# An LSTM kernel on one Trainium2 core: U sums on VectorE, bias differences in result buffers, streamed products from step 6, step 7's plain products ahead of step 0

## Chip, core and metric

The kernel runs on one core of one Trainium2 chip. The metric is the device time of one execution in microseconds (us), less is better. The kernel before takes 3121.33 us (median of three runs, 3120.87 to 3123.91).

In the profile PE is TensorE's matmul stream, PEld its weight loads, DVE is VectorE, ACT is ScalarE, POOL is GpSimd, and SPq is the queue of the Sync engine, from which every DMA of this kernel is issued. L245 is line 245 of the kernel before.

## What is computed

An LSTM over 512 steps, batch 32, input width and hidden width 512, all float32, with the input added to the output:

```python
def step(carry, xw_t):
    prev_h, prev_c = carry
    a = xw_t + prev_h @ Wh
    i = sigmoid(a[:, :Hd]); f = sigmoid(a[:, Hd:2*Hd])
    o = sigmoid(a[:, 2*Hd:3*Hd]); g = tanh(a[:, 3*Hd:])
    next_c = f * prev_c + i * g
    next_h = o * tanh(next_c)
    return (next_h, next_c), next_h

xW = einsum('ntd,dg->ntg', x, Wx) + b          # all steps: [32, 512, 2048]
hs = scan(step, (h0, 0), xW over the steps)
out = x + hs
```

So there are two products: the recurrent one, `prev_h @ Wh`, which must be made step by step, and the input product `x @ Wx`, which can be made at any time before its step.

## The kernel before, in words

**Layout.** A step's gates are a tile of 128 partitions (4 blocks of hidden units x 32 batch rows) by 512 columns, one PSUM bank. Eight banks are used: `xbank_0` to `xbank_4`, `bbank`, and `gbank_0`, `gbank_1`. From step 9 on a step's gates lie in `gbank[t % 2]`; the first nine steps have banks of a list (`bank_of`), step 7 has `xbank_3` and step 8 has `xbank_4`.

**A step.** `h_part(t)` (L245) adds the recurrent product to the step's bank. `cell(t)` reads the bank with ScalarE (L260 to L262), makes the new state on VectorE (L264 to L271, with a tanh of ScalarE, L267, between), transposes h for the next recurrent part (`ht`), and adds x for the output on GpSimd (L279). TensorE fills the time of the cell with input products.

**Input products, in two ways.** Steps 0 to 19 (the head, `HEAD = 20`) and the last 12 get *plain* products: x of one step against Wx as it is (`plain_block`, L178, 64 matmul rows for a step). Steps 20 to 499 are taken in 20 groups (`NG`) of 24 steps (`GS`), each with a fast bilinear scheme of 20 slots (`R`): each slot is a sum of x blocks (U) times a sum of weight blocks (V), seven 128x256 products a slot, and the results are added together to the outputs (W sums). These are the *streamed* products (`emit_matmuls`, L523). Their order is a list, `items`: row n of it has product 1 and 5 of slot n, 6 and 3 of slot n-1, 7 and 2 of slot n-2, and 4 of slot n-3. A position in the stream counts quarters of products, so 12 is three products; group 0 has 560.

- The U sums are made by `u_op` (L425) into six buffers `ubuf`, `u_ahead` deciding how far ahead. The sums of pairs of x blocks that they start from are made by `pair_sum` (L484 to L490) after `load_group` has brought a group's x into `xs0` or into `xs1`, which is the place of the weights Wx, free once the last plain product of the head is done.
- The V sums are made on VectorE in steps 0 to 4 (`v_slot`, L673), stored to DRAM (`v_store`, L685), and read back row by row into a ring of three (`load_v`, L602), two rows ahead of the stream. The buffers in which they are made are the ring itself and `ubuf`.
- Slot s uses bank `xbank[s % 5]` and half of `bbank`. Results are copied out by `evacuate` (ScalarE L569, L578, L585; VectorE L575, L579, L582) into eleven buffers `cbuf`, handed out from the list `free_c`. A product whose bank part has not been copied out yet has to wait (`needs`).
- The W sums (`w_op`, L389) are 1024 columns wide, in place in the `cbuf` buffers. A finished output block is stored to DRAM (L405) and read back into `xw` three steps before its step (`load_xw`, L614 and L620); `seed_step` (L631) copies it to the step's bank.
- Six slots (1, 3, 8, 11, 13, 17) start from a combination of biases: `seed_banks` (L553) copies it from a seed tile to the slot's bank. Two of the six combinations lie in `seeds_own`, the four others (`seeds[0]` to `seeds[3]`) in `r1[:, 6:8]`, the place of weights that plain products read.

**Where head plain products go.** Steps 0 to 4 are made before step 0 (`KEPT = 5`). The other 15 are made during steps 0 to 7 by the list `HEAD_PLAINS`, each ahead of its time. `keep(p)` adds the bias: in the bank itself, or into `xw[p % 3]`, or, from step 14 on, into one of six halves of `cbuf[8]` to `cbuf[10]` (`parks`), from which it is stored to DRAM (`kept_stores`, L784). The products of a step that has no bank of its own yet go to one of three banks in turn: `xbank_1`, `xbank_2`, `bbank` (`park_bank`).

**What sets the order.** The order on each engine is the order of the program text; nothing is reordered. In steps 0 to 15 (`HEAD_STEPS`) a step's work is a list of chunks, plain steps and pieces of the stream, and the cell is emitted after the first chunk. Jobs for VectorE (`jobs`) are spread over the plain chunks of their step. `room["dve"]` is a budget of VectorE time: TensorE's work adds to it, each operation takes its cost from it, and a W sum is emitted only while over 800 is left. SP issues its DMAs in program order too, and waits there for whatever the next one needs.

**The head before.** The stream begins in step 7, after the last plain step. U sums of the head and the pair sums of group 1 run on GpSimd. Raw biases are loaded in step 5 to three halves of `parks` (`load_raw_seeds`, L748); GpSimd takes their differences (L752) and, one step after the last plain product, makes three of the four late seeds in `r1[:, 6:8]` (L756 to L758), ScalarE copies the fourth (L759).

Of the kernel before, what the change touches and what calls it, by code (L numbers as in the profile page):

```python
# [28 lines left out]
TAU = (1, 0, 2)  # L29
NS = NG * R  # L30
KEPT = 5
STRAIGHT = 11
PARKED = 14
AHEAD = 28
STREAM0 = HEAD + GS - AHEAD
END = HEAD + GS * NG - AHEAD
SPLIT = END + 2
LATE = (454, 456, 458, 460, 462, 470, 471)

HEAD_PLAINS = ((14, 15), (6, 16), (5, 17), (7, 18), (8, 19), (11, 12), (9, 13), (10,))  # L40
V_DIRECT = (0, 2, 6, 9, 18, 19)
V_FIRST = (1,)
V_STEPS = ((3, 4, 5), (7, 8, 10), (11, 12, 13), (14, 15), (16, 17))
# [54 lines left out]
def kernel(  # L98
# [193 lines left out]

    free_c = [*range(8), 10, 8, 9]
    last_x = []
    free_u = list(range(6))
    room = {"dve": 0.0}
# [5 lines left out]
    def flat(a):  # L304
        return a.rearrange("p a b -> p (a b)")
# [110 lines left out]
    def u_block(gr, i):  # L416
        if i < 6:
            return flat(xs[gr.g % 2][:, i, 1:8])
        return flat(ubuf[:, gr.u[i]])

    def u_op(gr, terms):
        (a, sa), (b, sb) = sorted(terms.items(), key=lambda v: -v[1])
        dst = take(free_u)
        eng = nc.gpsimd if in_head[0] else nc.vector
        (eng.tensor_add if sb > 0 else eng.tensor_sub)(flat(ubuf[:, dst]), u_block(gr, a), u_block(gr, b))  # L425
        if not in_head[0]:
            room["dve"] -= cost_dve(896)
        for i in (a, b):
            if i > 5:
                gr.u_uses[i] -= 1  # L430
                if gr.u_uses[i] == 0:
                    free_u.append(gr.u[i])
        return dst

    u_made = [0]
    in_head = [True]

    def make_sum(gr, i):
        if i > 5 and i not in gr.u:
# [36 lines left out]
            in_=xg[g].rearrange("p (k s m) -> p k s m", k=6, s=4),  # L476
        )

    def pair_sum(g, i, eng=nc.vector):
        z = xs[g % 2]  # L480
        add, sub = eng.tensor_add, eng.tensor_sub
        a21, a11, a12, a22, s1, s2, s3, s4 = (z[:, :, n] for n in range(8))
        if i == 0:
            add(s1, a21, a22)  # L484
# [257 lines left out]
    def early_seeds():  # L742
        split_seeds((4, 5))
        sub(seeds[5], seeds[5], seeds[4])

    def load_raw_seeds():
        for i in range(3):
            nc.sync.dma_start(out=parks[i], in_=bias[i : i + 1].to_broadcast([P, W]))  # L748

    def split_raw_seeds():  # L750
        for q in parks[0:3]:
            nc.gpsimd.tensor_sub(q[:, HW:W], q[:, HW:W], q[:, 0:HW])  # L752

    def late_seeds():
        q = parks
        nc.gpsimd.tensor_add(seeds[3], q[2], seeds[4])  # L756
        nc.gpsimd.tensor_sub(seeds[2], q[2], q[0])
        nc.gpsimd.tensor_sub(seeds[1], q[1], q[0])  # L758
        nc.scalar.copy(seeds[0], q[0])  # L759

    parks = [cbuf[:, 8 + i // 2, i % 2 * 2 : i % 2 * 2 + 2].rearrange("p s c -> p (s c)") for i in range(6)]
    park_banks = [xbank[1], xbank[2], bbank]
# [7 lines left out]
        return park_banks[parked.index(p) % 3]  # L772

    def keep(p):
        if p < STRAIGHT:
            add(bank_of(p), bank_of(p), bias_full)
            return
        if p < PARKED:
            add(xw[:, p % 3], park_bank(p), bias_full)
            return  # L780
        n = p - PARKED
        dst = parks[n % 6]
        add(dst, park_bank(p), bias_full)
        kept_stores.append(lambda: nc.sync.dma_start(out=kept[n], in_=dst))  # L784

    with tc.manual_schedule():
# [4 lines left out]
        for c in range(4):  # L791
            ko, ki = divmod(c, 2)
            nc.sync.dma_start(
                out=r1[:, 4 * ko : 4 * ko + 4, 2 * ki : 2 * ki + 2].rearrange("p j s c -> p j (s c)"),
                in_=wx[c].rearrange("p (j c) -> p j c", j=NJ),
            )
        for j in range(NJ):
            nc.sync.dma_start(
                out=bias_full[j * B : (j + 1) * B], in_=bias[j : j + 1].to_broadcast([B, W])
            )  # L800
# [36 lines left out]
        HEAD_STEPS = STREAM0  # L837
        head_work = (HEAD - KEPT) * PLAIN + (R * 7) * PROD
        done_work = 0.0
        n_plain = 0  # L840
        group_loaded = 1
        plains_done = T
        s_done = {0: 4}
        v_ready = False
        plain_tail = []
# [4 lines left out]

        for t in range(T):
            h_part(t)
            for f in stores + kept_stores:
                f()
            stores.clear()
            kept_stores.clear()
            store_blocks()
            c, rest = divmod(t + 6, TC)
            if rest == 0 and 3 <= c < NCHUNK - 1:
# [9 lines left out]
            if t == 3:  # L869
                load_x(2, 4, 8)  # L870
                load_seeds(((4, 3), (5, 1)), nc.sync)
                load_group(0)
            if t == 5:
                load_raw_seeds()
            if PARKED <= t + 3 < HEAD + NG * GS:
                load_xw(t + 3)

            if t < HEAD_STEPS:
                target = head_work * (t + 1) / HEAD_STEPS
                chunks = []  # L880
                for p in HEAD_PLAINS[t] if t < len(HEAD_PLAINS) else ():
                    chunks.append(("plain", p))
                    n_plain += 1
                    done_work += PLAIN
                n = 4 * int((target - done_work) / PROD + 0.5) if n_plain == HEAD - KEPT else 0
                if t == HEAD_STEPS - 1 and n:
                    n = R * 7 * 4 - pos[0]
                left = n
                while left > 0:
                    m = min(left, 12 if chunks else 24)  # L890
                    chunks.append(("stream", m))
                    left -= m
                done_work += n * PROD / 4
                todo = jobs.pop(t, [])
                plains = sum(k == "plain" for k, _ in chunks)
                for i, (kind, m) in enumerate(chunks):
                    if kind == "plain":
                        bank = bank_of(m) if m < STRAIGHT else park_bank(m)
                        room["dve"] = 3000.0
                        for cc in range(4):  # L900
                            plain_block(m, cc, bank)
                        if i == 0:
                            cell(t)
                            if t + 1 >= STRAIGHT:
                                seed_step(t + 1)
                        keep(m)
                        if n_plain == HEAD - KEPT:
                            plains_done = t
                        last = i == plains - 1
                        for _ in range(len(todo) if last else -(-len(todo) // (plains - i))):  # L910
                            todo.pop(0)()
                            flush_v()
                    else:
                        load_v_ahead()
                        u_ahead(m)
                        if i == 0:
                            room["dve"] = min(room["dve"], 1000.0) + PLAIN
                        evacuate()
                        if t >= HEAD_STEPS - 3 and dve_jobs:
                            dve_jobs.pop(0)()  # L920
                        u_ahead(m + 24)
                        while wqueue and room["dve"] > 800:
                            w_op()
                        seed_banks(m)
                        emit_matmuls(m)
                        room["dve"] += m * PROD / 4
                        if i == 0:
                            cell(t)
                            room["dve"] -= 2500.0
                            if t + 1 >= STRAIGHT:  # L930
# [12 lines left out]

# [5 lines left out]
            in_head[0] = False  # L949
# [95 lines left out]
```

## Time and profile before

| | |
|---|---|
| three runs, median | 3121.33 us (3120.87 to 3123.91) |
| profiled execution | 3121.53 us, span 3119.80 us, mean granted TensorE clock 0.999 |
| PE busy over the span | 3094.5 us, 99% |
| DVE / ACT / POOL busy | 2226.7 (71%) / 1452.0 (47%) / 282.0 (9%) us |
| DMA | 760.39 MB, mean 244 GB/s |

How to read the profile's rows. A line of the page's busy time by stretches gives the stretch, its length, and for each engine the busy time with the number of instructions, then the granted clock of TensorE as a share of full speed, the busy share of the 16 DMA engines, and GB/s. A line of the waits gives who waited for whom: us in total, times, the longest. A line of the timeline gives the start, the busy time, the engine, the line and operation, what is written and read, and how many instructions are merged in it; brackets hold the idle time before it and what ended it. The end of a matmul row is modelled, so distances are better taken from start to start. A line of the groups gives busy time and mean duration in ns, then the idle time before. A float32 matmul is two rows in the trace.

### The profile page before, as it was taken

Reading aid. Unit: us, or ns where it says so; the run is one execution under the profiler, and the core shown is the slowest. Engines: PE = TensorE matmul, PEld = TensorE weight load, DVE = VectorE, ACT = ScalarE, POOL = GpSimd, SP = SyncE. Lnnn points to the kernel's source line nnn. Section 1 sums busy time; section 2 is a strip of 40 time slices with the busy share of each in tenths; the row PEclk is TensorE's granted clock in tenths of the full one; section 3 lists DMA queues with packets and bytes.
Section 4 is the critical chain, followed back from the end, with each engine's and each line's share of the span. In section 5 each row is a group of like instructions: output and inputs, shape, how many; then the busy total and the mean of one; then the engine's idle time right before and its main releaser. Section 6 shows DMA issues by size and latency. Waiting matters only on the chain.

```text
span 3119.8 us, 109182 instructions
## 1 busy us (share of the span) xinstructions
PE 3094.5 (99%) x44064; PEld 1660.0 (53%) x44064; DVE 2226.7 (71%) x6192; ACT 1452.0 (47%) x5484; POOL 282.0 (9%) x533
## 2 busy tenths in 40 slices
PE   9989999999999999999999999999999999999999
PEld 6544455555555555555555555555555555555576
DVE  6576777767676767777676767677776767677644
ACT  1244444444444444444444444444444444444444
POOL 0330000000000000000000000000000000000000
PEclk9999999999999999999999999999999999999999
DMA  9677778787877777787878777777878787878630
GB/s 349 239 265 247 254 246 274 233 262 240 261 243 262 246 249 255 247 274 230 262 241 260 245 260 247 249 255 246 273 232 261 239 261 245 260 248 275 202 91 22
DMA packets 307561, 760.39 MB, mean 244 GB/s; under 512 B 49008, under 2 KB 91760, under 8 KB 306544
## 3 DMA queue, kind: packets, MB, share of 16 engines
q1 hardware_dynamic: 307056, 753.40, 74.5%
q8 instruction: 348, 5.70, 0.8%
q14 instruction: 157, 1.29, 0.1%
HBM read 573.90 MB, written 179.31 MB: 241 GB/s over the span
## 4 chain that ended last, share of the span: by engine, by line
PE 94%; DVE 1%; issue 1%; ACT 0%; POOL 0%; DVEq 0%; ACTq 0%; POOLq 0%
PE gbank L245 53%; PE xbank L523 32%; PE bbank L523 5%; PE xbank L245 2%; PE xbank L187 1%; DVE cbuf L389 0%; DVE prod L264 0%; DVE s L265 0%; POOL ubuf L425 0%; ACT s L260 0%; DVE hbuf L269 0%; DVE ht L271 0%; ACT tanh_c L267 0%; POOL r L486 0%; ACT gbank L631 0%
## 5 line engine op out<-in xcount | busy, mean ns | idle before, releaser
L245 PE MATMUL gbank<-wh_sb,ht 128*32 128x512 f32 (+1 forms) x16224 | 1781.3, 577 | 2.7 <-DVE ht L271 1.1
L245 PEld LDWEIGHTS gbank<-wh_sb,ht 128*32 128x32 f32 x16224 | 608.8, 110 | 829.9 <-issue 708.6
L523 PE MATMUL xbank<-vring,ubuf 128*32 128x256 f32 (+1 forms) x15464 | 955.2, 364 | 6.2 <-POOL ubuf L425 3.2
L260 ACT ACTIVATE s<-gbank 128x128 f32<-128x128 f32 x976 | 273.6, 280 | 1284.2 <-PE gbank L245 1283.6
L523 PEld LDWEIGHTS xbank<-vring,ubuf 128*32 128x32 f32 x15464 | 585.3, 110 | 371.7 <-issue 190.6
L264 DVE TENSOR_TENSOR prod<-s 128x128 f32<-128x128 f32 x1024 | 295.2, 288 | 641.4 <-ACT s L261 641.3
L389 DVE TENSOR_TENSOR cbuf<-cbuf 128x1024 f32<-128x1024 f32 x408 | 503.2, 1246 | 1.7 <-ACT cbuf L585 0.2
L279 POOL TENSOR_TENSOR oc<-xnat,ht 128x128 f32<-128x128 f32 x504 | 232.2, 461 | 2796.3 <-DVE ht L271 1427.6
L267 ACT ACTIVATE tanh_c<-s 128x64 f32<-128x64 f32 x1024 | 262.6, 257 | 247.2 <-DVE s L265 244.6
L271 DVE STREAM_TRANSPOSE ht<-hbuf 128x64 f32<-128x64 f32 x1022 | 250.8, 245 | 74.4 <-DVE hbuf L269 0.9
L631 ACT COPY gbank<-xw 128x512 f32<-128x512 f32 x463 | 278.7, 602 | 0.1
L265 DVE TENSOR_TENSOR s<-prod 128x64 f32<-128x64 f32 x1024 | 230.3, 225 | 35.2
L569 ACT COPY cbuf<-xbank 128x512 f32<-128x512 f32 x374 | 218.6, 585 | 38.1 <-PE xbank L523 21.8
L269 DVE TENSOR_TENSOR hbuf<-o,tanh_c 128x64 f32<-128x64 f32 x1024 | 213.2, 208 | 28.3 <-ACT tanh_c L267 27.8
L261 ACT ACTIVATE s<-gbank 128x64 f32<-128x64 f32 x976 | 224.5, 230 | 0.0
L579 DVE TENSOR_TENSOR cbuf<-xbank,cbuf 128x256 f32<-128x256 f32 x374 | 153.3, 410 | 76.7 <-ACT cbuf L578 74.7
L523 PE MATMUL bbank<-vring,ubuf 128*32 128x256 f32 (+1 forms) x2704 | 200.1, 355 | 7.3 <-DVE cbuf L575 7.3
L523 PE MATMUL xbank<-vring,xs 128*32 128x256 f32 (+1 forms) x2472 | 172.9, 373 | 1.8 <-ACT xbank L553 1.8
L523 PE MATMUL xbank<-vring,r 128*32 128x256 f32 (+1 forms) x2480 | 173.2, 372 | 0.0
L262 ACT ACTIVATE o<-gbank 128x128 f32<-128x128 f32 (+1 forms) x507 | 153.2, 302 | 0.0
L582 DVE TENSOR_TENSOR cbuf<-xbank,cbuf 128x256 f32<-128x256 f32 x374 | 152.0, 406 | 0.0
L575 DVE TENSOR_TENSOR cbuf<-bbank,cbuf 128x256 f32<-128x256 f32 x374 | 151.5, 405 | 0.0
(113 smaller groups left out, 1828.4 us busy)
## 6 DMA issues: line engine op xcount, KB each, us to landing
vring<-vdram SPq DMA_DIRECT2D x340, 896.0 KB, 5.5
xw<-xwd SPq DMA_DIRECT2D x1920, 64.0 KB, 4.5
xwd<-cbuf SPq DMA_DIRECT2D x221, 512.0 KB, 4.3
out_dram<-oc SPq DMA_DIRECT2D x255, 128.0 KB, 3.6
xnat<-in_x_dram SPq DMA_DIRECT2D x62, 512.0 KB, 5.1
xs<-in_x_grouped_dram SPq DMA_DIRECT2D x10, 1536.0 KB, 8.8
vring<-vdram SPq DMA_DIRECT2D x20, 768.0 KB, 6.7
r<-in_x_grouped_dram SPq DMA_DIRECT2D x10, 1536.0 KB, 9.0
```

Of the source, the lines that this page charges most:

```text
L245: nc.tensor.matmul(dst[j * B : (j + 1) * B], state["ht"][:, k], m, start=False, stop=True, skip_group_check=True)
L260: nc.scalar.activation(s[:, u, 0:2], g[:, n_, 0:2], AF.Sigmoid)
L261: nc.scalar.activation(s[:, u, 2], g[:, n_, 3], AF.Tanh)
L264: nc.vector.tensor_mul(prod[:, u], s[:, u, 0:2], s[:, u, 2:4])
L265: add(nxt[:, u, 3], prod[:, u, 0], prod[:, u, 1])
L267: nc.scalar.activation(tanh_c[:, HALVES[u]], nxt[:, u, 3], AF.Tanh)
L271: nc.vector.transpose(ht[:, 2 * u : 2 * u + 2].rearrange("p q b -> p (q b)"), hbuf[:, HALVES[u]])
L279: (nc.gpsimd if t < T - 8 else nc.vector).tensor_add(oc[:, tt % 2], x_of(t), ht)
L389: op(c_of(dst), c_of(src), c_of(bb))
L523: nc.tensor.matmul(dst[j * B : (j + 1) * B, cols], left_of(gr, s, r)[:, j * B : (j + 1) * B], vring[:, row % 3, RIGHT[r], cols], start=sta ...
L569: nc.scalar.copy(t[:, 0:4:3], xb.rearrange("p (n c) -> p n c", n=2))
L631: nc.scalar.copy(bank_of(t), src)
```

## The change

- `u_op` and `pair_sum` always use VectorE, and the U sums of the head are taken from the budget.
- Step 7's plain products (`FIRST = 7`) are made before step 0; its x is loaded right after the weights. Step 7 is now one of the steps whose product is kept in `xw` and copied back (`SEEDED`).
- `HEAD_PLAINS` is another list: steps 5 and 6 have one plain step each, step 7 has two. The stream's quarters in each step are written out in `HEAD_STREAM` (32 in steps 6 and 7, then 56, 60, 60, and 64 in steps 11 to 15), in chunks of 12 between the plain steps, with a first chunk of 24, or 16 and 12 in steps 7 and 8, ahead of the cell.
- The raw biases are loaded in step 4 to `cbuf[6]` and `cbuf[7]`, which now come last in `free_c`. VectorE makes the differences there in step 6, and after the last plain product one DMA moves all four late seeds to `r1[:, 6:8]`.
- `early_seeds` is a job of step 4, the pair sums of group 0 and its first U sums are jobs of step 5.
- The stores of kept products all wait until step 6; `load_v_ahead` begins at the end of step 4; group 1 is loaded at the end of step 10. A W sum is also emitted without budget when fewer than three `cbuf` buffers are free.

```diff
-STRAIGHT = 11
 PARKED = 14
+SEEDED = (7, *range(11, T))
...
-HEAD_PLAINS = ((14, 15), (6, 16), (5, 17), (7, 18), (8, 19), (11, 12), (9, 13), (10,))
+FIRST = 7
+HEAD_PLAINS = ((14, 15), (6, 16), (5, 17), (18, 19), (8, 11), (12,), (13,), (9, 10))
+HEAD_STREAM = (0, 0, 0, 0, 0, 0, 32, 32, 56, 60, 60, 64, 64, 64, 64, 64)
+AHEAD_OF_CELL = {7: 16, 8: 12}
...
-    free_c = [*range(8), 10, 8, 9]
+    free_c = [*range(6), 8, 9, 10, 6, 7]
...
     def u_op(gr, terms):
...
-        eng = nc.gpsimd if in_head[0] else nc.vector
-        (eng.tensor_add if sb > 0 else eng.tensor_sub)(flat(ubuf[:, dst]), u_block(gr, a), u_block(gr, b))
-        if not in_head[0]:
-            room["dve"] -= cost_dve(896)
+        (add if sb > 0 else sub)(flat(ubuf[:, dst]), u_block(gr, a), u_block(gr, b))
+        room["dve"] -= cost_dve(896)
...
+    raw_seeds = [cbuf[:, 6 + i // 2, i % 2 * 2 : i % 2 * 2 + 2].rearrange("p s c -> p (s c)") for i in range(4)]
     def load_raw_seeds():
         for i in range(3):
-            nc.sync.dma_start(out=parks[i], in_=bias[i : i + 1].to_broadcast([P, W]))
-    def split_raw_seeds():
-        for q in parks[0:3]:
-            nc.gpsimd.tensor_sub(q[:, HW:W], q[:, HW:W], q[:, 0:HW])
+            nc.sync.dma_start(out=raw_seeds[i], in_=bias[i : i + 1].to_broadcast([P, W]))
     def late_seeds():
-        q = parks
-        nc.gpsimd.tensor_add(seeds[3], q[2], seeds[4])
-        nc.gpsimd.tensor_sub(seeds[2], q[2], q[0])
-        nc.gpsimd.tensor_sub(seeds[1], q[1], q[0])
-        nc.scalar.copy(seeds[0], q[0])
+        q = raw_seeds
+        for v in q[0:3]:
+            sub(v[:, HW:W], v[:, HW:W], v[:, 0:HW])
+        add(q[3], q[2], seeds[4])
+        sub(q[2], q[2], q[0])
+        sub(q[1], q[1], q[0])
+    def move_seeds():
+        whole = lambda t: t.rearrange("p a s c -> p (a s c)")
+        nc.sync.dma_start(out=whole(r1[:, 6:8]), in_=whole(cbuf[:, 6:8]))
...
     def keep(p):
-        if p < STRAIGHT:
+        if p not in SEEDED:
...
+        load_x(0, 5, 8)
         for j in range(NJ):
...
         load_x(1)
-        load_x(0, 5, 8)
...
+        for c in range(4):
+            plain_block(FIRST, c, park_bank(FIRST))
...
+        keep(FIRST)
...
-        jobs.setdefault(6, []).extend(
-            [lambda i=i: pair_sum(0, i) for i in range(4)]
-            + [early_seeds, split_raw_seeds, lambda: u_ahead(28)]
-        )
+        jobs[4].append(early_seeds)
+        jobs[5] = [lambda i=i: pair_sum(0, i) for i in range(4)] + [lambda: u_ahead(28)]
+        jobs[6] = [late_seeds]
...
-            for f in stores + kept_stores:
+            for f in stores + (kept_stores if t > 5 else []):
...
-            if t == 5:
+            if t == 4:
                 load_raw_seeds()
...
+                left = HEAD_STREAM[t]
                 chunks = []
...
+                if t >= len(HEAD_PLAINS) - 1:
+                    chunks.append(("stream", AHEAD_OF_CELL.get(t, 24)))
+                    left -= chunks[0][1]
+                while plain or left:
+                    if plain:
+                        chunks.append(plain.pop(0))
+                    m = min(left, 12)
+                    if m:
+                        chunks.append(("stream", m))
+                        left -= m
...
+                        if m == HEAD_PLAINS[-1][-1]:
+                            move_seeds()
...
-                        while wqueue and room["dve"] > 800:
+                        while wqueue and (room["dve"] > 800 or len(free_c) < 3):
                             w_op()
...
-                            if t == plains_done + 1:
-                                late_seeds()
-                if t >= 5:
+                if t >= 4:
                     load_v_ahead()
-                if t >= 10 and group_loaded == 1 and n_plain == HEAD - KEPT and not dve_jobs and not jobs:
+                if t == 10:
...
-                    dve_jobs += [lambda i=i: pair_sum(1, i, nc.gpsimd) for i in range(4)]
+                    dve_jobs += [lambda i=i: pair_sum(1, i) for i in range(4)]
```

More of the change, by code (lines that the diff above doesn't have):

```diff
@@ L435 @@
     u_made = [0]
-    in_head = [True]
     def make_sum(gr, i):
@@ L477, in load_group, with pair_sum @@
         )
-    def pair_sum(g, i, eng=nc.vector):
+    def pair_sum(g, i):
         z = xs[g % 2]
-        add, sub = eng.tensor_add, eng.tensor_sub
         a21, a11, a12, a22, s1, s2, s3, s4 = (z[:, :, n] for n in range(8))
@@ L830 @@
             jobs.setdefault(t, []).extend([lambda s=s: v_slot(s) for s in ss])
-        jobs.setdefault(6, []).extend(
-            [lambda i=i: pair_sum(0, i) for i in range(4)]
-            + [early_seeds, split_raw_seeds, lambda: u_ahead(28)]
-        )
+        jobs[4].append(early_seeds)
+        jobs[5] = [lambda i=i: pair_sum(0, i) for i in range(4)] + [lambda: u_ahead(28)]
+        jobs[6] = [late_seeds]
         dve_jobs = []
         HEAD_STEPS = STREAM0
-        head_work = (HEAD - KEPT) * PLAIN + (R * 7) * PROD
-        done_work = 0.0
         n_plain = 0
         group_loaded = 1
-        plains_done = T
         s_done = {0: 4}
@@ L852 @@
             h_part(t)
-            for f in stores + kept_stores:
+            for f in stores + (kept_stores if t > 5 else []):
                 f()
             stores.clear()
-            kept_stores.clear()
+            if t > 5:
+                kept_stores.clear()
             store_blocks()
@@ L878 @@
             if t < HEAD_STEPS:
-                target = head_work * (t + 1) / HEAD_STEPS
+                plain = [("plain", p) for p in (HEAD_PLAINS[t] if t < len(HEAD_PLAINS) else ())]
+                n_plain += len(plain)
+                left = HEAD_STREAM[t]
                 chunks = []
[L881 to L893, printed above, removed]
+                if t >= len(HEAD_PLAINS) - 1:
[8 more added lines that the diff above has]
+                        left -= m
+                assert t < HEAD_STEPS - 1 or sum(HEAD_STREAM) == R * 7 * 4
                 todo = jobs.pop(t, [])
@@ L897 @@
                     if kind == "plain":
-                        bank = bank_of(m) if m < STRAIGHT else park_bank(m)
+                        bank = park_bank(m) if m in SEEDED else bank_of(m)
                         room["dve"] = 3000.0
@@ L903 @@
                             cell(t)
-                            if t + 1 >= STRAIGHT:
+                            if t + 1 in SEEDED:
                                 seed_step(t + 1)
                         keep(m)
-                        if n_plain == HEAD - KEPT:
-                            plains_done = t
+                        if m == HEAD_PLAINS[-1][-1]:
+                            move_seeds()
                         last = i == plains - 1
@@ L929 @@
                             room["dve"] -= 2500.0
-                            if t + 1 >= STRAIGHT:
+                            if t + 1 in SEEDED:
                                 seed_step(t + 1)
-                            if t == plains_done + 1:
-                                late_seeds()
-                if t >= 5:
+                if t >= 4:
                     load_v_ahead()
-                if t >= 10 and group_loaded == 1 and n_plain == HEAD - KEPT and not dve_jobs and not jobs:
+                if t == 10:
                     assert not v_stores
@@ L948 @@
             n = target
-            in_head[0] = False
             wait_at_end[0] = t >= END - 2
```

## The prediction, made before the changed kernel ran

> **What bounds the kernel now.** I read the busy time by stretches first, cutting the span where TensorE's work changes: before the first recurrent step is through, plain products only, the first streamed products, the rest.
>
> ```profile
> 0.00:38.27 38.27, 35.59 (x528) 22.77 (x532) 20.09 (x31) 2.95 (x9) 0.66 (x5) 1.00 0.98 350
> 38.27:107.20 68.93, 68.93 (x1062) 48.30 (x1056) 51.81 (x104) 9.02 (x47) 9.85 (x11) 1.00 0.90 317
> 107.20:216.20 109.00, 93.52 (x1383) 44.40 (x1377) 71.00 (x149) 42.81 (x131) 46.54 (x29) 0.97 0.70 238
> 216.20:3119.80 2903.60, 2896.42 (x41108) 1544.50 (x41100) 2083.79 (x5911) 1397.25 (x5297) 224.91 (x488) 1.00 0.75 241
> ```
>
> The columns are stretch, length, busy PE, PEld, DVE, ACT, POOL, granted clock, DMA share and GB/s. From 216.20 on TensorE is busy 2896.42 of 2903.60 us, so nothing large can be won there. Between 107.20 and 216.20 it idles 15.5 us, and there the clock is below 1.00. Next I asked what ended PE's idle time over the span, and read PE's timeline at those places.
>
> ```profile
> PE bbank L523 <- DVE cbuf L575: 7.3, 3, 3.8
> PE xbank L523 <- POOL ubuf L425: 3.2, 2, 1.6
> PE xbank L523 <- ACT xbank L553: 2.4, 3, 1.0
> PE xbank L523 <- DVE cbuf L579: 2.4, 1, 2.4
> ```
>
> ```profile
> 26.36 2.83 PE L245 MATMUL gbank<-wh_sb,ht 128*32 128x512 f32 x24
> 30.09 1.07 PE L245 MATMUL gbank<-wh_sb,ht 128*32 128x512 f32 x8 [0.90 <-DMA wh_sb<-in_L_cond_Wh_dram]
> 31.34 7.18 PE L178 MATMUL xbank<-r,xnat 128*32 128x256 f32 x128 [0.19 <-DMA xnat<-in_x_dram]
> ...
> 83.07 7.16 PE L178 MATMUL xbank<-r,xnat 128*32 128x256 f32 x128
> 89.97 3.69 PE L245 MATMUL gbank<-wh_sb,ht 128*32 128x512 f32 x32
> ...
> 134.56 1.48 PE L523 MATMUL xbank<-vring,ubuf 128*32 128x256 f32 x24
> 135.86 3.62 PE L245 MATMUL gbank<-wh_sb,ht 128*32 128x512 f32 x32
> 139.29 1.05 PE L523 MATMUL xbank<-vring,ubuf 128*32 128x256 f32 x16
> ...
> 148.45 0.64 PE L523 MATMUL xbank<-vring,ubuf 128*32 128x256 f32 x8 [2.42 <-DVE cbuf L579]
> 148.91 5.31 PE L245 MATMUL gbank<-wh_sb,ht 128*32 128x512 f32 x32
> ...
> 164.14 0.64 PE L523 MATMUL bbank<-vring,ubuf 128*32 128x256 f32 x8 [2.68 <-DVE cbuf L575]
> ...
> 165.03 3.62 PE L245 MATMUL gbank<-wh_sb,ht 128*32 128x512 f32 x32
> ...
> 203.27 0.64 PE L523 MATMUL bbank<-vring,ubuf 128*32 128x256 f32 x8 [3.82 <-DVE cbuf L575]
> ...
> 204.16 5.31 PE L245 MATMUL gbank<-wh_sb,ht 128*32 128x512 f32 x32
> ```
>
> Unit prices, from start to start: two plain steps 89.97 - 83.07 = 6.90, so 3.45 each; a recurrent part (32 rows of L245) 139.29 - 135.86 = 3.43; three streamed products (24 rows of L523) 135.86 - 134.56 = 1.30, so 0.433 each. The stretch 107.20 to 216.20 holds the recurrent parts of steps 8 to 15 and all 20 x 7 = 140 products of group 0: 8 x 3.43 + 140 x 0.433 = 88.0 us of work in 109.0. **The loss is 21.0 us**: the four waits, 15.3; two recurrent parts at a low clock, 2 x (5.31 - 3.62) = 3.4; and 2.3 because a row's modelled end lies past the true one (134.56 + 1.48 is past 135.86), so each stall is some 0.25 longer than its bracket. At the start, recurrent part 0 takes 31.34 - 26.36 = 4.98 in place of 3.43: **1.55 us** lost to two loads. Everything that can be recovered is 22.6 us.
>
> **Why VectorE is late there.** One stall in the timeline of all engines, then the 1024-column sums in this stretch and in the long run:
>
> ```profile
> 196.35 2.11 POOL L425 TENSOR_TENSOR ubuf<-ubuf 128x896 f32<-128x896 f32 x1
> ...
> 197.20 5.35 DVE L389 TENSOR_TENSOR cbuf<-cbuf 128x1024 f32<-128x1024 f32 x2
> ...
> 198.42 3.05 POOL L425 TENSOR_TENSOR ubuf<-r 128x896 f32<-128x896 f32 x1
> ```
>
> ```profile
> L389 DVE TENSOR_TENSOR cbuf<-cbuf 128x1024 f32<-128x1024 f32 x20 | 36.4, 1827 | 0.4 <-ACT cbuf L585 0.2
> ...
> L389 DVE TENSOR_TENSOR cbuf<-cbuf 128x1024 f32<-128x1024 f32 x378 | 454.8, 1216 | 1.3
> ```
>
> Two sums that take 2.4 us alone take 5.35 while GpSimd makes U sums, the two engines taking turns; the copy-out of bbank (L575) is queued behind them and TensorE waits 3.82 us for it. Over 20 sums this is 20 x 0.61 = 12 us of VectorE time.
>
> **The change, part by part.** *U sums, pair sums of group 1, bias differences from GpSimd to VectorE.* Prices:
>
> ```profile
> L425 DVE TENSOR_TENSOR ubuf<-xs x81: 1070/1081/1083, 342.4 to 2760.3; 128x896 f32<-128x896 f32 x81
> ...
> L425 POOL TENSOR_TENSOR ubuf<-xs x9: 2092/2105/3092, 102.0 to 192.0; 128x896 f32<-128x896 f32 x9
> ```
>
> ```profile
> L484 DVE TENSOR_TENSOR xs<-xs x10: 937/940/1037, 97.8 to 2575.7; 128x768 f32<-128x768 f32 x10
> ```
>
> ```profile
> L579 DVE TENSOR_TENSOR cbuf<-xbank,cbuf 128x256 f32<-128x256 f32 x343 | 140.4, 409 | 65.3 <-ACT cbuf L578 63.6 <-DMA xw<-xwd 1.7
> ```
>
> VectorE gains about 15 U sums (13 for a group, the next group's first two), 15 x 1.08 = 16.2 us; four pair sums, 3.8; six late seed operations, three of 256 columns (nearest row L579, 0.41) and three of 512 (the 0.69 of L779 below), 3.3: 23.3 us, against 12 us of contention given back. The late seeds run in step 6 after its keep, before the first copy-out anyone needs (product (0,7), after recurrent part 7): about 3 us of cover, without it 3.3. Stalls that go: those on POOL (3.2), on VectorE (9.7), the low clock (3.4), and six of the nine modelled ends (1.5): 17.8.
>
> *Step 7's plain products ahead of step 0.* The 3.45 us only move, but recurrent part 0 then starts at 29.8, its last quarter of Wh is wanted at 32.4 (landed by 30.09), chunk 1 of x at 33.3 (by 31.34). The earlier load of x steps 5 to 7 puts 192 KB in front, 0.5 us at the 350 GB/s of the first stretch: still in time. Gain 1.55; with the cover gone, 0.
>
> *Stream from step 6.* With steps of 3.43 + 6.90 the recurrent parts stand at 40.1 (step 1), 81.5 (step 5), 88.4 (step 6, because step 5 has one plain step), and the first product at 95.3. Here a new wait appears. Step 5's jobs on VectorE are four pair sums and two U sums, queued ahead of step 6's cell:
>
> ```profile
> 83.78 0.29 DVE L264 TENSOR_TENSOR prod<-s 128x128 f32<-128x128 f32 x1 [1.08 <-ACT s L261]
> ...
> 85.44 0.24 DVE L271 STREAM_TRANSPOSE ht<-hbuf 128x64 f32<-128x64 f32 x1
> 86.82 0.69 DVE L779 TENSOR_TENSOR xw<-xbank,bias_full 128x512 f32<-128x512 f32 x1 [1.14 <-PE xbank L178]
> ```
>
> ```profile
> 158.44 0.59 ACT L553 COPY xbank<-r 128x512 f32<-128x512 f32 x1
> ```
>
> A cell starts on VectorE 0.7 us after its recurrent part and takes 1.9. Plain step 12 ends at 88.4, its keep at 89.4; 4 x 0.94 and 2 x 1.08 bring VectorE to 95.3, where cell 6 could have started at 92.6. The cell ends at 97.2, keep(13) at 97.9, and only then may ScalarE copy the seed of slot 1 into the same bank (xbank_1): 98.5. TensorE wants it for the third product at 96.2. **New wait 2.3 us**, between 0 (the jobs done early) and 5 (the V rows late too, a rival below). Step 7's recurrent part waits for nothing more.
>
> *SP's queue.* The six stores of kept products (1.5 MB, 4.2 us at 350 GB/s) leave the crowded stretch before 100 us and go out together in step 6, behind V rows 0 to 2 and ahead of V row 3, which is wanted after plain step 9 at 109.6: 2 to 3 us of cover. The one DMA of the seeds waits on SP until plain step 10 has read its weights, near 114.5; queued behind it are an output store and V row 6, wanted near 129. No row shows an SBUF to SBUF transfer of 1 MB; the nearest, from the page's list of DMA issues (count, size, median us to landing):
>
> ```profile
> xwd<-cbuf SPq DMA_DIRECT2D x221, 512.0 KB, 4.3
> ...
> xs<-in_x_grouped_dram SPq DMA_DIRECT2D x10, 1536.0 KB, 8.8
> ```
>
> Between 4 and 9 us it is there before 124, and slot 8's seed is wanted near 138. I take 0; with the cover gone, 1 to 2 us.
>
> *What stays.* Seed copies stand behind the cell and the copy-outs on ScalarE whatever the split; the three waits on L553 cost 2.4 + 0.8 = 3.2 now. I keep 3.2 (bounds 1.5 and 5): slots 11 and 13 now come just behind a cell again.
>
> *VectorE's new load.* A step of the late head streams 16 products: 6.9 VectorE copy-outs (three for every seven products) x 0.41, a cell of 1.9, up to 4 sums of 1.22, some 2 U sums of 1.08, together 11.8 at the worst against 3.43 + 16 x 0.433 = 10.4 us of TensorE; the planner's budget holds most sums back for the stretch after 216, where VectorE is 72% busy. Lower bound 0, upper 5 steps x 1.4 = 7. I take 2, near the lower, because the budget now counts the U sums.
>
> **Sum.** The profiled execution took 3121.53 us (span 3119.80), 0.2 above the median 3121.33. 3121.5 - 22.6 + 2.3 + 3.2 + 2 = **3106.4 us**; I forecast 3106.
>
> The 2.3 us wait may also cost clock. Here idle times of 2.42 and 3.82 us were followed by recurrent parts of 5.31 us, one of 2.68 was not (165.03). I put it at 0; it is 1.7 if it comes, and the time is then 3108. The Trainium skill, "TensorE: Matmul & The Clock Gate" (Part 1: The HAM clock gate), says the clock halves only after an idle window of about 3.4 us; by that rule a 2.3 us wait costs nothing and 3106 stands. The trace disagrees on the length: 2.42 us was enough.
>
> **The rivals.** *VectorE hides everything* (0 for its load, 1.5 of seed waits): 3121.5 - 22.6 + 3.8 = 3102.7. For it: no stall on VectorE in the 30 us from 107 where GpSimd had little to do. Against: the step's load above.
>
> *VectorE becomes the bound* of steps 10 to 15: 7 us in place of 2: 3111.4. For: 11.8 against 10.4. Against: the budget.
>
> *V rows come late.* They are written and read back through DRAM:
>
> ```profile
> 81.62 5.42 SPq L685 DMA_DIRECT2D vdram<-vring  x4
> ...
> 93.43 1.93 SPq L602 DMA_DIRECT2D vring<-vdram  x3
> ```
>
> ```profile
> vring<-vdram SPq DMA_DIRECT2D x340, 896.0 KB, 5.5
> ```
>
> The loads waited for the last store to land. If they again go out at 93.4 and land about 5.5 us on (the median row), the first product starts near 99 and the start costs 5 with row 1 behind it: 3109. Against: five stores of 256 KB fewer stand in front.
>
> *Slower.* The waits on VectorE come from queue order, not from GpSimd: then the 9.7 us stay, and every added operation stands in front of a copy-out. 9.7 + 1 for modelled ends, 23.3 added, 2.3, 3.2 and the clock's 3.4 are 42.9 against 22.6 recovered: 3142. It decides from the point at which the losses pass 22.6 + 6.2 = 28.8 us, that is once about a third of the added 23.3 us stands in front of copy-outs on top of the rest (42.9 - 23.3 = 19.6). Against: every long L389 has a GpSimd operation beside it, as above.
>
> *No gain:* SP's order or buffers running out take back 16 us or so, 3121; only their sum could do it.
>
> **How the numbers follow.** Forecast 0.50, hidden 0.15, VectorE bound 0.13, V late 0.09, no gain 0.05, slower 0.08. The first four give faster, 0.87. A measurement here cannot tell less than 0.2% (6.2 us) from no change, so same is 3115 to 3127.5. The range leaves out the last two and the edges: 3100 to 3113; the low end is the hidden case with the new wait gone too.
>
> **What would show it.** Right: recurrent part 0 without a gap; the first L523 near 95; one wait of about 2 us at the third product, put down to ScalarE's L553; L389 back at about 1.22 us before 200; the recurrent part of step 16 near 201 where it now starts at 216.2; the rest of the span unchanged. Wrong: waits on L575, L579 or L582 of over 5 us in steps 9 to 15 (VectorE bound), PE waiting for vring (V late), or a longer stretch after step 16 because sums were put off.

## The result, and the profile after

The changed kernel takes 3112.24 us (median of eight runs, 3110.83 to 3113.83) against 3120.77 us of the kernel before measured beside it: ratio 0.9972, 95% interval 0.9961 to 0.9983. That is 8.5 us less, more than the 0.2% that the prediction took as the least that can be told from nothing, and a little over half of the 15.3 us forecast (3106 against 3121.33). The profiled execution's span is 3110.9 us.

The busy time by stretches of the profile after, cut at its own recurrent parts (7 at 104.64, 11 at 147.74, 16 at 207.03; columns as before):

```profile
98.00:104.64 6.64, 4.67 (x57) 2.24 (x53) 3.18 (x7) 1.92 (x4) 0.00 (x0) 0.74 0.97 323
104.64:147.74 43.10, 43.10 (x676) 30.70 (x672) 23.30 (x63) 16.21 (x53) 1.83 (x4) 1.00 0.67 230
147.74:207.03 59.29, 53.01 (x806) 27.20 (x801) 49.34 (x102) 24.75 (x78) 2.28 (x5) 1.00 0.81 277
207.03:3110.90 2903.87, 2896.84 (x41108) 1549.04 (x41100) 2083.82 (x5912) 1397.15 (x5297) 224.83 (x488) 1.00 0.75 241
```

The recurrent part of step 16 starts 9.2 us earlier (207.03, was 216.20), and from there on both kernels are alike: 2903.87 against 2903.60 us. Steps 7 to 10 run without a gap. What is lost lies at the start of the stream and in steps 11 to 14. TensorE's timeline after, in those two places, every row with a wait and the rows between where they show the clock:

```profile
97.25 1.07 PE L522 MATMUL xbank<-vring,ubuf 128*32 128x256 f32 x16 [1.54 <-DMA vring<-vdram]
99.03 1.94 PE L522 MATMUL xbank<-vring,xs 128*32 128x256 f32 x16 [0.71 <-ACT cbuf L568]
100.71 1.80 PE L522 MATMUL xbank<-vring,ubuf 128*32 128x256 f32 x16
103.78 1.07 PE L522 MATMUL xbank<-vring,ubuf 128*32 128x256 f32 x16 [1.26 <-DMA vring<-vdram]
...
155.77 1.07 PE L522 MATMUL xbank<-vring,xs 128*32 128x256 f32 x16 [0.90 <-ACT xbank L552]
...
159.76 0.64 PE L522 MATMUL xbank<-vring,ubuf 128*32 128x256 f32 x8 [0.77 <-DMA vring<-vdram]
...
167.71 1.93 PE L522 MATMUL xbank<-vring,ubuf 128*32 128x256 f32 x32 [1.28 <-ACT xbank L552]
...
180.56 0.64 PE L522 MATMUL xbank<-vring,ubuf 128*32 128x256 f32 x8 [1.45 <-DVE cbuf L578]
...
195.80 0.64 PE L522 MATMUL bbank<-vring,ubuf 128*32 128x256 f32 x8 [1.87 <-DVE cbuf L574]
```

*The start.* Recurrent part 6 starts at 88.57 and part 7 at 104.64: 16.07 us for 10.34 of work (3.43 + 3.45 + 8 x 0.433), a loss of 5.7. It comes from the arrival of three V rows, and the clock falls there too: the first product was due at 95.45 and starts at 97.25 (1.8), the third was due at 98.1 and starts at 99.03 (0.9), the seventh waits until 103.78. In between, the two products of the row at 99.03 take 100.71 - 99.03 = 1.68 us where they should take 0.87: half speed. The stretch from 99.00 to 102.50 has a granted clock of 0.54:

```profile
99.00:102.50 3.50, 3.47 (x32) 1.58 (x32) 1.79 (x3) 0.58 (x1) 0.00 (x0) 0.54 0.91 298
```

Four products at half speed take 1.7 us more, and 1.3 us remain for the seventh's wait. But at full speed the seventh product would still have waited for its row until 103.78, so the low clock cost nothing here, and the rows alone account for the 5.7 us. The Sync queue shows why the rows come late:

```profile
85.12 3.71 SPq L684 DMA_DIRECT2D vdram<-vring  x4
94.56 1.28 SPq L601 DMA_DIRECT2D vring<-vdram  x3
95.93 0.38 SPq L286 DMA_DIRECT2D out_dram<-oc  x1
96.36 3.99 SPq L784 DMA_DIRECT2D kept<-cbuf  x6
```

The three loads go out at 94.56, when the last store from the ring has landed, 1.1 us later than in the kernel before (93.43), though the first product is now due 12 us earlier. Their landing took 2.6, 4.0 and 8.2 us (the shortest, middle and longest of the three in the view of that line): 97.2, 99.0, 103.7, the very times at which TensorE goes on. The timeline puts the second wait down to ScalarE's L568, but in e3 below the third product starts at 98.24, while that copy is still running (98.12, for 0.58 us): it does not need it, and what landed at this moment is the second row.

*Steps 11 to 14.* Their starts, 147.74, 160.19, 172.05, 184.27 and 196.69, are 12.45, 11.86, 12.22 and 12.42 us apart in place of 10.36: 7.5 us. The five brackets, each with the 0.25 us of a modelled end, make this up: 2.7 for two seed copies, 1.0 for a V row, 3.8 for two copy-outs on VectorE. The 1024-column sums are back at their own time (profile after, groups from 104.64 to 207.03):

```profile
L392 DVE TENSOR_TENSOR cbuf<-cbuf 128x1024 f32<-128x1024 f32 x19 | 22.7, 1217 | 0.2
```

But they now come in runs, four at 171.12 and three at 191.59 (VectorE's timeline after). The second run stands right ahead of the copy-out that TensorE wants. The first pushes back a pair sum, a U sum and the cell of step 13, which starts at 177.96 although ScalarE has its first gates ready at 176.12; ScalarE's copies wait for that cell, and the copy-out of 180.08 for them:

```profile
171.12 5.06 DVE L392 TENSOR_TENSOR cbuf<-cbuf 128x1024 f32<-128x1024 f32 x4
...
180.08 0.42 DVE L578 TENSOR_TENSOR cbuf<-xbank,cbuf 128x256 f32<-128x256 f32 x1 [0.23 <-ACT cbuf L577]
...
191.59 3.48 DVE L392 TENSOR_TENSOR cbuf<-cbuf 128x1024 f32<-128x1024 f32 x3
195.00 0.41 DVE L581 TENSOR_TENSOR cbuf<-xbank,cbuf 128x256 f32<-128x256 f32 x1
195.33 0.41 DVE L574 TENSOR_TENSOR cbuf<-bbank,cbuf 128x256 f32<-128x256 f32 x1
```

### The profile page after: what moved, and what is told of

The parts are those of the page before. It is cut to its first block, busy times and chain, and to the rows that moved or that the text cites. A ratio compares the mean times of both kernels' runs of the same rounds, so it can differ in the third digit from the quotient of the medians.

```text
span 3110.9 us, 109178 instructions
## 1 busy us (share of the span) xinstructions
PE 3092.5 (99%) x44064; PEld 1674.5 (54%) x44064; DVE 2229.6 (72%) x6217; ACT 1451.8 (47%) x5484; POOL 232.3 (7%) x508
## 4 chain that ended last, share of the span: by engine, by line
PE 93%; DVE 1%; ACT 0%; issue 0%; ACTq 0%; DVEq 0%
PE gbank L248 53%; PE xbank L522 32%; PE bbank L522 5%; PE xbank L248 2%; PE xbank L190 1%; DVE cbuf L392 0%; DVE prod L267 0%; DVE s L268 0%; ACT s L263 0%; DVE hbuf L272 0%; ACT tanh_c L270 0%; DVE ht L274 0%; DVE cbuf L578 0%; ACT cbuf L584 0%; DVE ubuf L427 0%
## 5 line engine op out<-in xcount | busy, mean ns | idle before, releaser
L392 DVE TENSOR_TENSOR cbuf<-cbuf 128x1024 f32<-128x1024 f32 x408 | 490.3, 1215 | 1.5
L568 ACT COPY cbuf<-xbank 128x512 f32<-128x512 f32 x374 | 218.5, 584 | 43.4 <-PE xbank L522 22.2
```

The source lines that it names most:

```text
L392: op(c_of(dst), c_of(src), c_of(bb))
L568: nc.scalar.copy(t[:, 0:4:3], xb.rearrange("p (n c) -> p n c", n=2))
```

## The experiments

Two questions: which part of the change earns the time, and what gives half of it back. Where a kernel ran only once, the verdict rests on the starts of the recurrent parts in its trace (7: 104.64 and 16: 207.03 in the changed kernel). Recurrent part 6 starts within 0.9 us of 88.57 in all variants of the changed kernel. From part 6 to part 7 the changed kernel takes 16.07 us, and e6 and e7, whose edits lie behind that stretch, 16.73 and 16.71: differences of under about 0.7 us there cannot be told apart.

**e1, the U sums back on GpSimd.**

```diff
-        (add if sb > 0 else sub)(flat(ubuf[:, dst]), u_block(gr, a), u_block(gr, b))
-        room["dve"] -= cost_dve(896)
+        eng = nc.gpsimd if in_head[0] else nc.vector
+        (eng.tensor_add if sb > 0 else eng.tensor_sub)(flat(ubuf[:, dst]), u_block(gr, a), u_block(gr, b))
+        if not in_head[0]:
+            room["dve"] -= cost_dve(896)
...
```

> The changed kernel with the head's U sums back on GpSimd (and out of the budget); all else as changed. Theory, taking turns: GpSimd's U sums hold up VectorE's 1024-column sums, so those go from a mean of 1.217 us back to 1.5 or more before step 16, TensorE waits for U sums or copy-outs again, and recurrent part 16 starts at 212 to 216 in place of 207.0. Rival, order: the gain came from the new order of the stream alone and VectorE is relieved of 11 operations; recurrent part 16 then starts at 207 or earlier.

Measured: 3121.47 us beside 3119.28 of the kernel before; recurrent part 16 at 215.44. The gain is gone. In the trace of this run VectorE's sums are slow again beside U sums of GpSimd:

```profile
197.30 2.10 POOL L428 TENSOR_TENSOR ubuf<-ubuf 128x896 f32<-128x896 f32 x1
...
198.14 5.35 DVE L392 TENSOR_TENSOR cbuf<-cbuf 128x1024 f32<-128x1024 f32 x2
...
199.36 3.05 POOL L428 TENSOR_TENSOR ubuf<-r 128x896 f32<-128x896 f32 x1
...
203.75 0.41 DVE L577 TENSOR_TENSOR cbuf<-bbank,cbuf 128x256 f32<-128x256 f32 x1
```

The mean of the 1024-column sums is 1.636 us. The rival, that the new order earns the time, falls.

**e8 and e11, the U sums alone.** The kernel before with this one part of the change. Without a rule that forces sums when buffers run short there are not enough buffers, so e8 forces at fewer than two free ones, e11 at fewer than three as the change does.

```diff
 (in the kernel before)
-        eng = nc.gpsimd if in_head[0] else nc.vector
-        (eng.tensor_add if sb > 0 else eng.tensor_sub)(flat(ubuf[:, dst]), u_block(gr, a), u_block(gr, b))
-        if not in_head[0]:
-            room["dve"] -= cost_dve(896)
+        (add if sb > 0 else sub)(flat(ubuf[:, dst]), u_block(gr, a), u_block(gr, b))
+        room["dve"] -= cost_dve(896)
...
-                        while wqueue and room["dve"] > 800:
+                        while wqueue and (room["dve"] > 800 or len(free_c) < 2):
```

> The kernel before with only the head's U sums on VectorE, in the budget (and a W sum out of budget when fewer than two buffers are free, without which the buffers do not last). Theory, taking turns: this alone brings the greater part: the 1024-column sums before step 16 fall from a mean of 1.83 to 1.2 to 1.35 us, the low clock at 149 and 204 goes, recurrent part 16 starts at 203 to 208 in place of 216.2, time 3108 to 3113. Rival: without the new order VectorE's own load makes the waits; recurrent part 16 stays at 212 or later.

> As e8, the kernel before with only the U sums on VectorE, but W sums forced out of budget at fewer than three free buffers, as in the changed kernel. Theory: the threshold of three makes runs of W sums in a row here too, so recurrent part 16 comes 1 to 3 us after the 199.07 of e8, time 3105 to 3107. Rival: the threshold only hurts together with the changed kernel's smaller chunks; recurrent part 16 within 0.5 us of 199.07.

Measured: e8 takes 3103.93 us, ratio to the kernel before 0.9947 (0.9933 to 0.9961), recurrent part 16 at 199.07: 17.1 us earlier than before, and 8 us earlier than with the whole change, so the U sums earned more than expected. The mean of its 1024-column sums is 1.219 us (104 to 200). e11 takes 3104.92 us, 0.9952 (0.9939 to 0.9966), with part 16 at 200.31, 1.2 us behind e8 as expected. The two times cannot be told apart, but the trace of e11 has a wait that e8 has not, of the size and on the operation seen in the changed kernel:

```profile
189.08 0.64 PE L521 MATMUL bbank<-vring,ubuf 128*32 128x256 f32 x8 [1.86 <-DVE cbuf L573]
```

Of e8's waits in the stream three are over 0.2 us, none behind a VectorE copy-out:

```profile
151.83 1.07 PE L521 MATMUL xbank<-vring,xs 128*32 128x256 f32 x16 [0.98 <-ACT xbank L551]
...
162.41 1.93 PE L521 MATMUL xbank<-vring,ubuf 128*32 128x256 f32 x32 [0.50 <-ACT xbank L551]
...
175.76 2.37 PE L521 MATMUL xbank<-vring,ubuf 128*32 128x256 f32 x40 [0.65 <-ACT cbuf L583]
```

So one part of the change earns about twice what the whole does, and the rest costs some 8 us (6.7 against e11, which forces sums by the same rule as the change).

**e2, e3, e4, e5: the start of the stream.** Three edits, one by one and together.

```diff
 (e2: the stores of kept products one step later)
-            for f in stores + (kept_stores if t > 5 else []):
+            for f in stores + (kept_stores if t > 6 else []):
...
 (e3: V sums of slots 14 and 15 in the ring, those for 16 and 17 in U buffers)
+        if s == 14:
+            free_v.sort(key=[2, 0, 3, 4, 5].index)
...
-    free_u = list(range(6))
+    free_u = [4, 5, 0, 1, 2, 3]
...
 (e4: cell 6 ahead of all U sums)
-        jobs[5] = [lambda i=i: pair_sum(0, i) for i in range(4)] + [lambda: u_ahead(28)]
-        jobs[6] = [late_seeds]
+        jobs[5] = [lambda i=i: pair_sum(0, i) for i in range(4)]
+        jobs[6] = [lambda: u_ahead(28), late_seeds]
...
                             cell(t)
+                            if t == 6:
+                                u_ahead(4)
```

> The changed kernel with the six stores of kept products one step later (step 7). Theory, shared DMA: V row 2 lands late (103.7) because these stores share the DMA engines with it; it lands near 101, the products 7 and 8 start at once after product 6, and recurrent part 7 starts at 103.3 in place of 104.64. Rival: the row is late only because it was issued late (94.6); recurrent part 7 stays at 104.6.

> The changed kernel with the last two V sums (slots 16, 17) made in other buffers than the ring, so that V rows 0 to 2 do not wait for their stores to land (U sums begin in other buffers for that). Theory, V rows late: the rows are issued near 89 in place of 94.6, the first streamed product starts at 95.45 in place of 97.25, the third waits for the seed copy until 98.4 to 98.6, and recurrent part 7 starts at 101.0 (if the clock stays) to 102.7 (if it halves again), not at 104.64. Rival, VectorE's queue alone: the third product was late because of the step 5 jobs and V rows hide behind that; recurrent part 7 moves by under 0.5 us.

> The changed kernel with cell 6 ahead of the first two U sums on VectorE. Theory, V rows late: they set the start, so recurrent part 7 stays within 0.5 us of 104.64. Rival, VectorE's queue: the seed copy comes 1.2 us earlier (97.2) and recurrent part 7 with it, near 103.4.

> The three start edits together: stores of kept products in step 7, other buffers for the last V sums, cell 6 ahead of the U sums. Theory: V rows and the cell's place each hide the other, so the sum is more than its parts: third product near 97.2, waits under 1 us, the clock stays at 1.00, recurrent part 7 at 99.5 to 100.5 in place of 104.64, recurrent part 16 at 202 to 203, time 3107 to 3108. Rival: the gain is given back in steps 11 to 15, where VectorE or the buffers set the pace; recurrent part 16 stays above 205.

| | time, one run | recurrent part 7 | from part 6 to 7 | recurrent part 16 |
|---|---|---|---|---|
| changed kernel | 3112.24 (median) | 104.64 | 16.07 | 207.03 |
| e2, stores later | 3111.60 | 103.01 | 14.72 | 205.99 |
| e3, V rows not held up | 3108.92 | 100.86 | 12.50 | 203.49 |
| e4, cell first | 3112.34 | 104.48 | 15.50 | 206.78 |
| e5, all three | 3107.99 | 100.17 | 12.01 | 202.59 |

e3 brings part 7 3.8 us forward with the V rows alone, e4 wins nothing that can be told apart: the late rows set the start. In e2 the third row lands in 6.4 us in place of 8.2, as if the six stores had slowed it. But with the stores where the change has them the same row takes 6.6 us in e1, 7.2 in e4, 7.8 in e7 and 8.1 in e6, so this is suggested and not shown. e3 also uncovers the wait that was forecast, at the place and nearly the moment forecast; its 12.50 us are 2.2 over the 10.34 of work:

```profile
98.24 1.07 PE L522 MATMUL xbank<-vring,xs 128*32 128x256 f32 x16 [1.87 <-ACT xbank L552]
```

With all three edits the longest wait left at the start is 0.88 us and the granted clock stays at 1.00. Against e3 that is 0.5 us more from part 6 to 7 (0.8 in e9, which starts alike): about the scatter, and the runs do not say which of the two other edits earns it.

**e7 and e9, forcing sums at fewer than two free buffers.**

```diff
-                        while wqueue and (room["dve"] > 800 or len(free_c) < 3):
+                        while wqueue and (room["dve"] > 800 or len(free_c) < 2):
```

> The changed kernel with W sums forced out of budget only when fewer than two buffers are free, not three. Theory, buffer shortage: the runs of three and four 1024-column sums in a row (191.6 and 171.1) shrink by one and go later, and the waits of 1.87 and 1.45 us behind them by about 1.2 each; recurrent part 16 at 205 to 206. Rival, VectorE simply has too much to do in steps 12 to 15: the sums move and the waits move with them; recurrent part 16 within 0.5 us of 207.0.

> The three start edits and the forcing of W sums at fewer than two free buffers together. Theory, the two losses lie in different steps: the gains add up, 4.4 + 2.8: recurrent part 16 at 199.5 to 200.5, time near 3105. Rival: the earlier start moves the buffer shortage with it; recurrent part 16 above 202.

Measured: e7 3109.72 us, recurrent part 16 at 204.26, better than expected: the waits of 1.45 and 1.87 us are gone altogether, not shortened. e9, with the edits of e5 as well: 3104.15 us, part 16 at 198.86. The two losses add up: from part 7 to part 16 the changed kernel and e5 take 102.4 us, e7 and e9 99.3.

**e6, e10, e12: ScalarE's queue, and group 1's load.** e6 copies the next step's gates at the end of the step. e10 is e9 with those copies after the third chunk and seed copies ahead of copy-outs; e12 is e10 with group 1 loaded earlier.

```diff
 (e6)
                             room["dve"] -= 2500.0
-                            if t + 1 in SEEDED:
-                                seed_step(t + 1)
...
+                if t > 6 and t + 1 in SEEDED:
+                    seed_step(t + 1)
...
 (e10)
+                        if not any(r == 4 for _, r in finished[:1]):
+                            seed_banks(m)
                         evacuate()
...
-                            if t + 1 in SEEDED:
-                                seed_step(t + 1)
+                        if i == (2 if t > 7 else 0) and t + 1 in SEEDED:
+                            seed_step(t + 1)
...
 (e12, on top of e10)
-                if t == 10:
+                if t == 8:
```

> The changed kernel with the copy of the next step's gates (L630) at the end of each stream step instead of right behind the cell. Theory, ScalarE's queue: the seed copies of slots 11 and 13 come 0.5 us earlier, the two waits of 0.90 and 1.28 us shrink to 0.4 and 0.8, recurrent part 16 at 206.0. Rival: those copies wait for the last product of the chunk before, not for the queue; recurrent part 16 stays at 207.0.

> As the run before, and on ScalarE the seed copies ahead of copy-outs where their bank is free, and the next step's gates copied after the third chunk of a step in place of the first. Theory, ScalarE's queue: the waits of 0.90 and 1.28 us on the seed copies fall to 0.4 and 0, recurrent part 16 another 1.5 to 2 us earlier, at 198 to 199, time 3103 to 3104. Rival: copy-outs behind the seed copies come later and TensorE waits for those; no gain over the run before.

> As e10, with the load of group 1 at the end of step 8 in place of step 10. Theory: the 1.49 us wait for V row 11 in e10 comes from the 1.5 MB of that load on the DMA engines ahead of it, and goes: recurrent part 16 at 195 to 195.5 in place of 196.8, time 3101. Rival: the row is late because SP issues it behind the store of an output block; the wait stays and so does recurrent part 16.

Measured: e6 3113.91 us, part 16 at 208.19, a miss: one seed wait went and the other shrank to 0.97, but recurrent parts 13 and 14 then waited 0.77 and 0.55 us for the late gates. Of the 1.2 us by which part 16 is later, 0.9 lie ahead of part 7, where the edit changes nothing; behind it the edit wins nothing. e10 takes 3102.57 us, 0.9945 (0.9932 to 0.9959), part 16 at 196.81: no wait on a seed copy is left, one of 1.49 us for a V row, in step 11, is new. e12 takes 3101.86 us, 0.9943 (0.9929 to 0.9956), part 16 at 195.99; that wait stays at 1.32, so group 1's load is not its cause, and most of the 0.8 us by which part 16 comes earlier lies ahead of part 7 (98.93 against 99.59):

```profile
153.79 0.64 PE L522 MATMUL xbank<-vring,ubuf 128*32 128x256 f32 x8 [1.32 <-DMA vring<-vdram]
```

The trace of e10 fits the rival: the row is issued at 147.62 and lands 7.0 us later, and ahead of it on SP stands the store of an output block, issued at 147.14 after SP had waited 4.6 us for it. No run moved that store. e10 and e12 beat both kernels; against e8 their intervals overlap.

## Why the prediction was right in kind and mis-sized

The time lies in the range, 0.8 us from its upper end, and nearer to two rivals (V rows late, 3109; VectorE the bound, 3111.4) than to the forecast: the first came whole and the second in part. That the range holds their sum is owed to its width as much as to the reasoning.

*The waits on POOL and VectorE and the low clock, 17.8 us: right.* e8 shows the term nearly by itself, 17.1 us: with the U sums gone from GpSimd the 1024-column sums fall from 1.827 to 1.219 us, though the pair sums and bias differences stay there; e1 shows the reverse. The rule by which e8 forces sums does not earn this, since e1 has such a rule too. The slower rival, queue order without GpSimd, falls with it. One ground given for the rival *VectorE hides everything* was misread: in the 30 us from 107 GpSimd was busy for 16.2 us, so that stretch says little of VectorE without it.

*Step 7's plain products, 1.55: right.* Steps 0 and 1 of the profile after begin at 29.98 and 40.33, without a gap: 10.35 us in place of 11.91.

*The new wait, 2.3: the step that failed most; 5.7 measured.* The reasoning on VectorE's queue was sound, and its size too (2.2 us in e3). What failed is that the V rows were taken to be there in time: held as a rival with a chance of 0.09 and 5 us, they were the later of the two. The rival's own number, loads at 93.4 and a first product near 99, was close; I dismissed it because five stores of kept products no longer stand in front. They do not, but that did not help: the last four stores from the ring leave SP from 85.12 to 88.0, later than before (81.62 to 85.9). In front of them now stand the three raw bias loads, on SP until 83.3, and the V sums that they store end at 83.36 (before: 82.70). The view of SP's waits puts the 1.8 us from 83.3 to 85.1 down to the landing of earlier stores from `ubuf`; no run tried this. The six stores moved to step 6 go out right behind V rows 0 to 2, as said; they were costed at nothing against V row 3 alone, and what they cost V row 2 is open (e2).

*The clock, put at 0 with 1.7 named as the price: it came, and cost nothing, because the third row came later still.* The Trainium skill ("TensorE: Matmul & The Clock Gate", Part 1: The HAM clock gate) has the clock halve after an idle window of about 3.4 us, and the prediction set the length of single waits against this. Neither the length of a wait nor the sum of two decides in these runs. In the changed kernel waits of 1.8 and 0.9 us with 0.9 us of work between them were followed by a granted clock of 0.54; in e2, at the same place, 2.4 and 0.6 us were not (1.00 from 97.50 to 103.00). In e1 a wait of 3.81 us was followed by a recurrent part at full speed, and one of 2.06 by one of 5.31 us.

*Seed copies, 3.2: 2.7 measured, right.* Slots 11 and 13, as said; e10 shows ScalarE's order to be the cause.

*VectorE's load, 2: 3.8 measured.* The ground for the low value, a budget that counts the U sums, failed: the change also lets a sum through without budget at fewer than three free buffers, and I took that for a safeguard. With the budget spent it became the rule: counted in the program as it is built, 12 of the 19 sums ahead of step 16 go out with the budget at 800 or less, among them three of the four at 171.12 and all three at 191.59. e7 removes both waits with one digit. A V row that came late in step 11 cost a further 1.0, which no term had.

The sum by its terms: 22.6 recoverable, less 5.7, 2.7, 3.8 and 1.0, is 9.4; the trace has 9.2 at step 16 and 8.9 over the span.

## What to carry to other kernels

A bundle that wins can hold a part that wins twice as much: put the one part that removes the named cause into the old kernel by itself before the schedule around it is rewritten. When work is started earlier, go through every input it needs back to the instruction that makes it ready, and do not let a wait found on one queue stand for all of them: the later one hides the earlier, and an edit on the hidden one shows nothing. A fallback in a planner deserves to be costed as if it were the rule once the budget ahead of it is loaded further.

## What had not been expected of the hardware

The third V row, 768 KB, took 6.6 to 8.2 us to land in five runs with 1.5 MB of stores issued just behind it, and 6.4 in the one run with those a step later: a spread of 1.6 us where the program text orders the same transfers, nearly the whole of e2's difference. In the changed kernel a halving of the clock followed 2.7 us of waiting spread over two pieces in 3.6 us, and lasted 3.4 us; in e2 3.0 us in two pieces, and in e1 a single wait of 3.81, did not bring it.
